# One level of Strassen's scheme for the W product of a conv, low-rank and dense layer, with a reordered opening

## The chip, the cores and the metric

The kernel runs on one core of a Trainium2 chip. The metric is the device time of one execution in microseconds, as the median of several runs. A profile is one execution recorded by the hardware profiler; its span goes from the first to the last instruction on the core.

## The reference

Everything is fp32. A grouped 1-d conv over 64 samples of 64 channels and 1024 positions (4 groups, 16 channels in and out of each, 9 taps, padding 4) gets a term of the condition and a bias; the result, taken as 8 batches of 512 rows of 1024, goes through a dense layer with two low-rank updates, and the input is added.

```python
z   = conv(x, weight) + (cond @ c_weight.T)[:, :, None] + fside[None, :, None]   # (64, 64, 1024)
A   = einsum('bn,nri->bri', gate, lora_A)      # 8 batches, 16 loras, rank 32
B   = einsum('bn,nor->bor', gate, lora_B)
out = x + z @ kernel + bias \
        + (z @ A[b].T) @ B[b].T \
        + (z @ lora_A_shared.T) @ lora_B_shared.T
```

## The kernel before

**Split operands.** TensorE works on fp32r operands. To keep fp32 accuracy each operand is split into a high part (ScalarE copies it into an fp32r tile, `hi_of`, line 104) and a low part (what is left, a subtraction with two SBUF inputs on VectorE or GpSimd, `lo_of`, line 109). A product is three matmuls: high by high, high by low, low by high.

**Tiles.** A row tile is two samples, 128 rows; there are 32, four to a batch. For each tile `load` brings the input in blocks of eight positions, `xhi` and `xlo` split it, `conv` (line 141) runs 24 matmuls of 256 columns, `evac` (VectorE line 159, or ScalarE line 155) adds the condition on the way out of PSUM, `turned` (line 164) transposes 32 by 32 blocks on VectorE so that positions lie on partitions, and `yhi` and `ylo` split the result.

**The W product.** `product` (line 301) multiplies a tile by W in three accumulators of 352, 320 and 352 columns, eight blocks of 128 positions each, three matmuls per block: 72 matmuls. The middle accumulator also carries the 32 rank columns of the batch's low-rank A, so all 72 are 352 wide. The shared low-rank update is folded into W at the start (`fmm`, line 215, on TensorE; `fadd`, line 219, on VectorE).

**The low-rank update of a batch.** `lora_out` copies the 32 rank columns out of PSUM, `turn` (line 312) transposes them on TensorE, `axhi` and `axlo` split them, and `delta` (line 326) adds their product with B, and the bias, to each accumulator. `total` (line 333) adds the residual on VectorE, and `store` writes the tile.

**The mixing of the loras.** A and B of a batch are sums over 16 loras weighted by the gate. `mix` (line 250) does one lora by one VectorE instruction that reads two SBUF tensors; in the opening part of it goes over ScalarE (`gmul`, line 257) and GpSimd (`gadd`, line 261). For each later batch 32 such steps are spread over the tiles of the batch before. B then goes through DRAM (`pbput`, lines 280 and 281, on GpSimd's queue).

**Order.** Each engine issues in program order. Up to the fourth tile the order is the list START, in which W, the loras and the first samples arrive piece by piece. From tile 4 on a loop emits, for tile i, the conv of tile i+1, the store of tile i-1, products, deltas and totals. All loads go over SyncE's queue, the stores over ScalarE's.

Of the kernel before, what the change touches and what calls it, by code (L numbers as in the profile page):

```python
# [8 lines left out]
F32 = mybir.dt.float32  # L9
F32R = mybir.dt.float32r  # L10
ALU = mybir.AluOpType
ACTF = mybir.ActivationFunctionType
PSUM = bass.MemoryType.PSUM

P = 128
NS, C, L = 64, 64, 1024          # samples, channels, length
G, CG, OG, KW = 4, 16, 16, 9     # conv groups, channels in / out of a group, taps
D = 1024                         # output features
NB, NL, R = 8, 16, 32            # batches, loras, rank
NT = NS // 2                     # row tiles: two samples, 128 rows each  # L20
BT = NT // NB                    # row tiles of a batch
JB = 129                         # blocks of 8 positions, half a block off, with padding
CH = ((0, 352), (352, 320), (672, 352))   # columns of W in a tile's three accumulators
CA = 1                           # the accumulator that also carries the lora's R columns
DS = 3 * R                       # rows of the split lora product
NBIAS = 2
NAX = 4
NSTART = 4                       # tiles that the steps of START cover
E = mybir.EngineType
ORDERED = (E.PE, E.SP, E.DVE, E.Activation, E.Pool)  # L30
AW = 8 * R                       # one lora on a partition: 8 x R of A, or 256 of B


# The steps up to the fourth tile, in the order in which each engine issues them: W, the loras and
# the first samples arrive, are split, and are used piece by piece.
START = """
warm, sbload 0, busy 15, busy 6, sbhi 0, sblo 0 v, saload, sahi, cwload, cwide, eye, busy 6, load 0 0 2,
xhi 0 0 2, small 0, twload 2, twload 0, ctload, xlo 0 0 2 p, thi 2, salo, fmm 0 1 m, load 0 2 2, sbload 1,
load 1, thi 0, tlo 0 v, cmul, small 1, xhi 0 2 2, wload 0 0, wload 0 6, wload 0 2, wload 0 4, tlo 2 v,
wload 2 2, xlo 0 2 2 v, small 2, fmm 0 7 m, sbhi 1, sblo 1 p, conv 0 0, conv 0 1, wload 2 6, conv 0 2, xhi 1,  # L40
csum, fmm 0 4 m, evac 0 0 0, conv 0 3, evac 0 1 1, xlo 1 0 4 p, load 2, fmm 0 3 m, wload 2 0, fmm 0 0 m,
fmm 2 6 m, turned 0 0, yhi 0 0 64, fadd 0 1, fadd 0 0, whi 0 0, wload 1 0, fmm 0 6 c, fadd 0 6, ylo 0 0 64 p,
fadd 0 7, lload 0 0 8, fmm 2 0 m, fadd 0 3, whi 0 6, fmm 0 2 c, fadd 0 2, whi 0 2, conv 1 0, turned 0 1,
yhi 0 64 64, wload 2 4, ones, fadd 0 4, fmm 0 5 m, fadd 0 5, fmm 2 7 m, conv 1 1, ylo 0 64 64 p, conv 1 2,
conv 1 3, wload 1 2, whi 0 4, evac 1 0 1, fmm 2 3 m, fmm 1 3 m, wlo 0 0 v, product 0 0 0 2, fadd 2 6,
wlo 0 2 v, fmm 2 5 c, lload 0 8 8, wload 1 6, product 0 0 2 2, fmm 1 1 c, evac 1 1 1, fmm 2 2 m, bihi, xhi 2,
wlo 0 4, wlo 0 6 p, product 0 0 4 2, fadd 2 7, wload 1 4, fmm 2 4 m, xlo 2 0 4 p, product 0 0 6 2, turned 1 0,
turned 1 1, fadd 2 0, yhi 1, fadd 2 3, fadd 1 1, ylo 1 0 128 v, bilo, fmm 2 1 m, fmm 1 0 c, fadd 2 1, whi 2 0,
product 1 0 0 1, fadd 1 0, fadd 2 2, product 1 0 1 2, fmm 1 7 m, mix 0 0 0, mix 0 0 1, product 1 0 3 2,
conv 2 2, product 1 0 5 2, fadd 2 4, product 1 0 7 1, mix 0 0 2, fadd 2 5, fmm 1 2 m, conv 2 0, whi 2 2,  # L50
wlo 2 0 p, product 0 2 0 1, mix 0 0 3, conv 2 1, product 0 2 1 1, whi 2 4, product 1 2 0 1, mix 0 0 4,
lload 1 0 8, mix 0 0 5, fadd 1 3, mix 0 0 6, whi 2 6, fadd 1 2, whi 1 2, evac 2 0 0, conv 2 3, mix 0 0 7,
fadd 1 7, product 1 2 1 1, wlo 2 4 p, mix 0 0 8, wlo 2 2 p, product 0 2 2 1, fmm 1 6 m, mix 0 0 9, mix 0 0 10,
mix 0 0 11, mix 0 0 12, product 1 2 2 1, mix 0 0 13, fmm 1 5 c, wlo 1 2 p, whi 1 0, fadd 1 5, load 3,
wlo 2 6 p, wlo 1 0 p, mix 0 0 14, product 1 2 3 2, gmul 0 1 0, gmul 0 1 3, load 4, mix 0 0 15, fmm 1 4 m,
fadd 1 4, product 0 2 3 5, product 1 2 5 1, fadd 1 6, gmul 0 1 2, gmul 1 1 5, pahi 0, product 1 2 6 2,
palo 0 p, biput 0 1, product 0 1 0 1, xhi 3, residual 0, whi 1 4, mix 1 0 0, total 0 2, mix 1 0 1, gmul 0 1 4,
gmul 0 1 1, wlo 1 4 p, gmul 0 1 5, gmul 0 1 6, product 1 1 0 1, product 0 1 1 2, whi 1 6, xlo 3 0 4 v,
gadd 0 1 1 p, product 1 1 1 2, lload 1 8 8, mix 1 0 2, product 0 1 3 1, product 1 1 3 2, gadd 0 1 2 p,
wlo 1 6 v, evac 2 1 1, turned 2 1, gmul 0 1 10, product 0 1 4 1, product 1 1 5 1, gadd 0 1 3 v,  # L60
product 1 1 6 2, turned 2 0, gmul 0 1 14, gmul 0 1 15, yhi 2, gmul 0 1 8, conv 3 0, conv 3 2, total 0 0,
conv 3 3, gadd 0 1 4 p, gadd 0 1 5 p, gmul 0 1 7, gadd 0 1 6 p, conv 3 1, product 0 1 5 1, gmul 0 1 12,
gmul 0 1 9, gadd 0 1 7 p, product 0 1 6 1, mix 1 0 3, ylo 2 0 128 v, gadd 0 1 8 v, residual 1, product 2 2 0 2,
gmul 1 1 7, product 0 1 7 1, gmul 0 1 11, product 2 1 0 1, mix 1 0 4, product 2 1 1 2, biput 1 1, evac 3 0 0,
product 2 1 3 1, gadd 0 1 9 p, product 2 2 2 3, lora_out 0, turn 0, gmul 0 1 13, product 2 1 4 3,
product 2 0 0 1, gadd 0 1 10 p, gadd 0 1 11 p, evac 3 1 0, turned 3 1, product 2 0 1 1, product 2 1 7 1,
turned 3 0, lora_out 1, gadd 0 1 12 v, gmul 1 1 1, total 0 1, yhi 3, gadd 0 1 13 v, xhi 4, gadd 0 1 14 v,
mix 1 0 5, ylo 3 0 128 p, gmul 1 1 6, product 2 0 2 1, product 2 2 5 1, gadd 0 1 15 v, total 1 1, pbhi 0,
mix 1 0 6, mix 1 0 7, pblo 0 v, axhi 0, axlo 0, mix 1 0 8, mix 1 0 9, gmul 1 1 3, turn 1, total 1 2,
mix 1 0 10, mix 1 0 11, gmul 1 1 4, product 3 1 0 1, gmul 1 1 2, pbput 0, axhi 1, product 3 1 1 1, axlo 1,  # L70
total 1 0, product 3 1 2 1, mix 1 0 12, product 2 2 6 1, product 3 2 0 2, product 2 0 3 1, lora_out 2,
product 3 1 3 1, biput 0 0, product 3 1 4 1, product 2 0 4 1, turn 2, gmul 1 1 0, gmul 1 1 8, axhi 2,
gmul 1 1 14, mix 1 0 13, xlo 4 0 4 v, residual 2, conv 4 0, gmul 1 1 9, gmul 1 1 10, load 5, xhi 5,
product 3 1 5 3, lora_out 3, conv 4 1, gadd 1 1 1 p, gadd 1 1 2 v, gadd 1 1 3 v, gadd 1 1 4 v, gadd 1 1 5 v,
mix 1 0 14, mix 1 0 15, pahi 1, gmul 1 1 13, product 2 0 5 2, axlo 2, product 2 0 7 1, product 2 2 7 1,
delta 2 2, delta 2 0, gadd 1 1 6 p, gadd 1 1 7 p, gmul 1 1 12, gadd 1 1 8 p, conv 4 2, delta 2 1, total 2 0,
total 2 2, product 3 2 2 1, delta 1 2 0, total 1 2, gadd 1 1 9 p, gadd 1 1 10 p, biput 1 0, product 3 0 0 2,
total 2 1, delta 0 1 0, gmul 1 1 11, gadd 1 1 11 p, product 3 0 2 1, gadd 1 1 12 p, gadd 1 1 13 p, gmul 1 1 15,
gadd 1 1 14 p, evac 4 0 1, turn 3, conv 4 3, product 3 0 3 1, axhi 3, axlo 3, turned 4 0, product 3 0 4 1,
delta 3 1, gadd 1 1 15 p, product 3 0 5 1, store 2, delta 0 0 0, total 0 0, pbhi 1, pblo 1 v, product 3 2 3 1,  # L80
evac 4 1 1, product 3 2 4 3, residual 3, turned 4 1, xlo 5 0 4 p, total 3 1, total 0 1, delta 0 2 0, total 0 2,
delta 1 0 0, total 1 0, palo 1 p, pbput 1, yhi 4, product 3 0 6 1, store 0, ylo 4 0 128 v, product 3 2 7 1,
delta 3 2, delta 1 1 0, total 1 1, store 1, total 3 2, product 3 0 7 1, delta 3 0, total 3 0
"""


@with_exitstack
def adaln_ffn(ctx: ExitStack, tc: tile.TileContext, xt, x, tw, w0, w1, w2, la, lb, gt,
              las, lbs, cw, ct, fs, bias, out):
    nc = tc.nc  # L90
    wsrc = (w0, w1, w2)

    const = ctx.enter_context(tc.tile_pool(name="const", bufs=1))
    pcv = ctx.enter_context(tc.tile_pool(name="pcv", bufs=2, space=PSUM))
    pmm = ctx.enter_context(tc.tile_pool(name="pmm", bufs=6, space=PSUM))
    raw = ctx.enter_context(tc.tile_pool(name="raw", bufs=7))
    dram = ctx.enter_context(tc.tile_pool(name="dram", bufs=2, space=bass.MemoryType.DRAM))
    work = ctx.enter_context(tc.tile_pool(name="work", bufs=2))

    def f32(t):  # L100
        return t.bitcast(F32)

    def hi_of(dst, src):
        nc.scalar.copy(dst, src)  # L104

    engs = {"v": nc.vector, "p": nc.gpsimd}

    def lo_of(dst, src, hi, eng="v"):
        engs[eng].tensor_tensor(dst, src, f32(hi), ALU.subtract)  # L109
# [431 lines left out]
```

## Time and profile before

| | |
|---|---|
| time, median of 3 runs | 513.43 us (512.79 to 513.49) |
| span of the profiled execution | 510.9 us |
| its own time | the page gives the span alone; the median of the runs is 2.5 us above it |
| TensorE busy | 497.0 us (97%), granted clock 0.997 |
| VectorE busy | 351.6 us (69%) |
| ScalarE, GpSimd busy | 120.8 and 130.1 us |
| DMA | 67.11 MB, mean 131 GB/s |
| W product, line 301 | 3 x 768 matmuls of 352 columns |
| conv, line 141 | 3 x 256 matmuls of 256 columns |

Busy times of matmuls overlap, since they are pipelined: what one costs is read from the distance between the starts of two.

### The profile page before, as it was taken

To read this page: it belongs to the slowest core of one execution; us is meant where nothing else is said; L and a number is where in the kernel's file an instruction comes from. 1 tells how busy PE (TensorE), PEld (TensorE's weight loads), DVE (VectorE), ACT (ScalarE), POOL (GpSimd) and SP (SyncE) were. 2 spreads that over 40 slices of the span, in tenths; PEclk is the share of its full clock that TensorE was granted. 3 is DMA by queue.
4 is the path that set the end of the run, shared out by engine and by line. 5 is a ranking of instruction groups with operands and counts; after the bars stand their busy time and mean duration, and the time that the engine had idled before them with its cause. 6 is when DMAs were issued, how large, how long until landed. Compare 5 with 4: busy or idle time off the path is not lost.

```text
span 510.9 us, 7936 instructions
## 1 busy us (share of the span) xinstructions
PE 497.0 (97%) x3259; PEld 491.2 (96%) x3259; DVE 351.6 (69%) x572; ACT 120.8 (24%) x221; POOL 130.1 (25%) x93
## 2 busy tenths in 40 slices
PE   8887989999999999999999999999999999999997
PEld 8776989999999999999999999999999999999996
DVE  5999896987737876577846878388864779544321
ACT  5733845111111112101221110211121011211000
POOL 4956538210121113011121102211120111310100
PEclk9998999999999999999999999999999999999999
DMA  8884223813442323333251234322153323441111
GB/s 269 329 335 171 85 87 122 293 77 125 154 156 84 123 83 148 123 125 124 83 182 66 105 125 156 131 107 107 64 181 126 123 84 125 143 166 42 41 42 41
DMA packets 20083, 67.11 MB, mean 131 GB/s; under 512 B 3104, under 2 KB 3840, under 8 KB 19536
## 3 DMA queue, kind: packets, MB, share of 16 engines
q1 hardware_dynamic: 13408, 43.47, 24.4%
q10 hardware_dynamic: 4752, 16.78, 8.2%
q0 software_dynamic: 1888, 6.36, 3.5%
q8 instruction: 25, 0.41, 0.3%
q14 instruction: 10, 0.08, 0.0%
HBM read 46.67 MB, written 19.92 MB: 130 GB/s over the span
## 4 chain that ended last, share of the span: by engine, by line
PE 82%; DVE 6%; POOL 4%; DMA 3%; issue 2%; SPq 2%; ACT 1%; POOLq 0%; ACTq 0%
PE mm L301 63%; PE cv L141 15%; PE mm L326 3%; DMA bst<-bih 2%; DVE eff L250 2%; POOL wl L109 1%; POOL xl L109 1%; DMA sbr<-in_dram 1%; DVE xr L333 1%; DVE z L164 1%; POOL eff L261 1%; PE pt L312 1%; DVE v L159 0%; DVE yl L109 0%; DVE eff L261 0%
## 5 line engine op out<-in xcount | busy, mean ns | idle before, releaser
L301 PE MATMUL mm<-wh,yh 128*128 128x352 f32 x768 | 250.9, 327 | 4.0 <-ACT wh L104 2.8
L301 PE MATMUL mm<-wl,yh 128*128 128x352 f32 x768 | 248.9, 324 | 0.8 <-POOL wl L109 0.8
L301 PE MATMUL mm<-wh,yl 128*128 128x352 f32 x768 | 248.7, 324 | 0.0
L301 PEld LDWEIGHTS mm<-wh,yh 128*128 128x128 f32 x768 | 144.9, 189 | 5.9 <-ACT wh L104 3.1
L301 PEld LDWEIGHTS mm<-wl,yh 128*128 128x128 f32 x768 | 145.0, 189 | 1.8 <-POOL wl L109 1.7
L301 PEld LDWEIGHTS mm<-wh,yl 128*128 128x128 f32 x768 | 144.8, 189 | 0.1
L250 DVE SCALAR_TENSOR_TENSOR eff<-lora,gat,eff 128x256 f32<-128x256 f32 x210 | 140.3, 718 | 0.5
L109 POOL TENSOR_TENSOR xl<-xt,xh 128x1032 fp32r<-128x1032 f32 (+1 forms) x30 | 74.9, 2497 | 249.8 <-ACT xh L104 249.7
L333 DVE TENSOR_TENSOR xr<-mm,xr 128x352 f32<-128x352 f32 (+1 forms) x96 | 46.3, 509 | 77.4 <-PE mm L326 77.4
L104 ACT CAST yh<-z 128x1024 fp32r<-128x1024 f32 (+1 forms) x33 | 33.8, 1025 | 240.8 <-DVE z L164 240.8
L159 DVE TENSOR_TENSOR v<-cv,cadd 128x512 f32<-128x512 f32 x58 | 40.0, 690 | 20.6 <-PE cv L141 20.4
L141 PE MATMUL cv<-xl,th 128*128 128x256 f32 x256 | 51.6, 282 | 1.6 <-DVE xl L109 1.0
L141 PE MATMUL cv<-xh,th 128*128 128x256 f32 x256 | 51.6, 283 | 0.7 <-DVE wr L219 0.7
L141 PE MATMUL cv<-xh,tl 128*128 128x256 f32 x256 | 51.4, 282 | 0.0
L164 DVE STREAM_TRANSPOSE z<-v 128x512 f32<-128x512 f32 x64 | 45.2, 709 | 2.1 <-ACT v L155 0.2
L109 DVE TENSOR_TENSOR yl<-z,yh 128x1024 fp32r<-128x1024 f32 x30 | 37.6, 1253 | 13.0 <-ACT yh L104 12.5
L141 PEld LDWEIGHTS cv<-xh,th 128*128 128x128 f32 x256 | 40.9, 189 | 1.3 <-DVE wr L219 1.2
L141 PEld LDWEIGHTS cv<-xl,th 128*128 128x128 f32 x256 | 39.5, 189 | 2.0 <-DVE xl L109 1.3
L141 PEld LDWEIGHTS cv<-xh,tl 128*128 128x128 f32 x256 | 39.5, 189 | 0.0
L104 ACT CAST xh<-xt 128x1032 fp32r<-128x1032 f32 (+1 forms) x33 | 33.9, 1027 | 1.1 <-DMA xt<-in_dram 1.1
L109 DVE TENSOR_TENSOR axt<-pt,axt 32x128 fp32r<-32x128 f32 x32 | 9.2, 288 | 28.1 <-ACT axt L104 27.5
L326 PE MATMUL mm<-bst,axt 98*128 98x352 f32 (+1 forms) x90 | 24.0, 319 | 0.2 <-DVE axt L109 0.2
(56 smaller groups left out, 216.1 us busy)
## 6 DMA issues: line engine op xcount, KB each, us to landing
xr<-in_dram SPq DMA_DIRECT2D x32, 512.0 KB, 4.4
xt<-in_dram SPq DMA_DIRECT2D x31, 516.0 KB, 3.6
out_dram<-xr ACTq DMA_DIRECT2D x31, 512.0 KB, 2.6
lora<-in_dram SPq DMA_DIRECT2D x4, 1024.0 KB, 6.3
bsc<-bhl POOLq DMA_DIRECT2D x8, 384.0 KB, 3.8
bst<-bsc POOLq DMA_DIRECT2D x8, 384.0 KB, 3.5
wr<-in_dram SPq DMA_DIRECT2D x8, 352.0 KB, 7.3
wr<-in_dram SPq DMA_DIRECT2D x4, 320.0 KB, 3.2
```

What stands on the lines that cost most here:

```text
L104: nc.scalar.copy(dst, src)
L109: engs[eng].tensor_tensor(dst, src, f32(hi), ALU.subtract)
L141: nc.tensor.matmul(cps[i, hf][:, gg], a[:, kt, g, :], b[:, g, :, kt:kt + P], start=(n == 0), stop=(n == len(prods) - 1))
L159: nc.vector.tensor_tensor(v[:, g0:g0 + 2], ps, c.unsqueeze(3).to_broadcast([P, 2, 2, P]), ALU.add)
L164: nc.vector.transpose(z[:, :, hf * 64:hf * 64 + 64].rearrange("p k (m o) -> p m k o", o=OG), v[:, g0:g0 + 2].rearrange("p g n j -> p (g n ...
L250: nc.vector.scalar_tensor_tensor(e, lora[w][:, n], gat[:, n, b:b + 1], e, ALU.mult, ALU.add)
L261: engs[eng].tensor_tensor(e, e, gated.pop((b, w, n)), ALU.add)
L301: nc.tensor.matmul(ps[:, :m], a[:, k, :], b[c][:, k, :m], start=(k == 0 and q == 0), stop=(k == 7 and q == 2))
L312: nc.tensor.transpose(pts[i], axs.pop(i).rearrange("p a r -> p (a r)"), ident)
L326: nc.tensor.matmul(acc[i, c][:, :n], axt[i % NAX], bst[(i // BT) % 2][:, c0:c0 + n], start=not more, stop=True, skip_group_check=bool(more))
L333: nc.vector.tensor_tensor(o, acc.pop((i, c))[:, :n], o, ALU.add)
```

## The change

**Pairs and blocks.** Two row tiles form a pair. The 256 by 1024 matrix of a pair and the 1024 by 1024 W are cut into 2 by 2 blocks, and the eight block products become seven (Winograd's variant): four sums of blocks of the pair (`asum`, GpSimd), four of W, made once (`wsum`, both engines), and seven products (`prod`), each four blocks of 128 positions by three matmuls of 512 columns. The products accumulate in four PSUM banks; three times a bank is copied out in between (`keep`, ScalarE), and the copies are added to the residual (`xsum`, `ysum`, `radd`, `yadd`) before `total`. All seven left and seven right blocks are split into high and low parts.

**The rest.** `conv` takes a pair and one group at a time, 512 columns instead of 256. The low-rank input is computed turned: the batch's A is the stationary operand and 128 positions by 128 rows of the pair the moving one (`lora`), so the TensorE transpose goes, and the accumulators carry no rank columns. The gate's mixing is done once at the start for all batches: per lora tensor eight fp32 matmuls with a masked gate (`gmask`, `mix`), copied out by ScalarE (`mixout`), written to DRAM (`mixput`) and read back per batch (`aload`, `bload`). GpSimd's queue issues only two small loads. Loads and stores become smaller and more.

**Order.** One list, ORDER, of 1657 steps replaces START and the loop. In its opening (up to `prod 2 0`) the seven products of pairs 0 and 1 are cut into single blocks and follow the arrival and preparation of W.

```diff
-CH = ((0, 352), (352, 320), (672, 352))   # columns of W in a tile's three accumulators
+A11, A12, S1, S3, A22, S2, S4 = range(7)
+B11, B21, T1, T3, N4, T2, B22, B12 = range(8)
+PRODUCTS = ((A11, B11, "a"), (A12, B21, "a"), (S1, T1, "d"), (S3, T3, "c"), (A22, N4, "c"), (S2, T2, "b"),
+            (S4, B22, "d"))
+ORDER = """
+warm, twload 0, gload, small 1, busy 26, saload 0, twload 1, small 0, xload 0 0, cwload, ctload, xload 0 1,
...
+conv 1 3, gmask, xhi 2 0, turned 1 0, wsum 3 2 p, wload 6 0, prod 0 3 0 1 0, evac 1 2 v, whi 3 2, wload 7 0,
+turned 1 1, xlo 2 0 p, prod 0 3 1 1 0, xhi 2 1, turned 1 2, evac 1 3 a, xload 2 2, conv 2 0, fadd 4 0,
+wlo 3 2 p, lload 0 2, wsum 3 3 v, mix 0 0, evac 2 0 a, fadd 6 0, xlo 2 1 p, prod 0 3 2 1 0, fadd 5 0, whi 3 3,
...
+rload 5 1, asum 5 5, delta 4 1, keep 5 0, lora 5 0, total 4 1, delta 4 3, asum 5 6, yhi 5 4, conv 6 0,
+total 4 3, store 4 1, rload 5 3, ylo 5 4 v, store 4 3, prod 5 1, xhi 6 2, evac 6 0 v, xlo 6 2 v, turned 6 0,
+xload 7 0, bload 3 0, lora 5 1, conv 6 1, yhi 5 5, bload 3 1, ylo 5 5 v, prod 5 2, xhi 6 3, evac 6 1 v,
+xlo 6 3 v, turned 6 1, xload 7 1, lora 5 2, keep 5 2, conv 6 2, yhi 5 6, ylo 5 6 v, prod 5 3, xhi 7 0,
+evac 6 2 v, xlo 7 0 v, turned 6 2, xload 7 2, conv 6 3, yhi 6 0, keep 5 3, ylo 6 0 v, lora 5 3, ysum 5 v,
+xhi 7 1, prod 5 4, axlow 5, evac 6 3 v, xlo 7 1 p, ahi 3, axsum 5, turned 6 3, axhi 5, xload 7 3, axlo 5,
+alo 3 p, prod 5 5, yhi 6 1, asum 6 2, aload 4, ylo 6 1 v, asum 6 3, delta 5 0, yhi 6 2, xsum 5, prod 5 6,
+adiff 4 p, total 5 0, radd 5 2 v, radd 5 1 p, store 5 0, radd 5 3 v, delta 5 2, ylo 6 2 v, yadd 5 p, yhi 6 3,
...
+    def conv(p, g):
+        h, l = xsp.pop((p, g))
+        ps = cps[p, g] = pcv.tile([P, 4, P], F32, tag="cv", name=f"cv{p}_{g}")
+        prods = [(kt, a, b) for a, b in ((th, h), (tl, h), (th, l)) for kt in range(2)]
+        for n, (kt, a, b) in enumerate(prods):
+            nc.tensor.matmul(ps, a[:, kt, g, :], b[:, :, kt:kt + P],
+                             start=(n == 0), stop=(n == len(prods) - 1))
...
+    def asum(p, b, eng="p"):
+        t = raw[p, b] = slot("s", f"s{b}_{p}", (P, HK, P))
+        m, n, op = {S1: (quarter(p, 1, 0), quarter(p, 1, 1), ALU.add),
+                    S2: (raw.get((p, S1)), quarter(p, 0, 0), ALU.subtract),
+                    S3: (quarter(p, 0, 0), quarter(p, 1, 0), ALU.subtract),
+                    S4: (quarter(p, 0, 1), raw.get((p, S2)), ALU.subtract)}[b]
+        engs[eng].tensor_tensor(t, m, n, op)
...
+    def wsum(b, k, eng="p"):
+        t = wr[b, k] = piece(f"ws{b}_{k}")
+        m, n = {T1: (B12, B11), T3: (B22, B12), T2: (B22, T1), N4: (B21, T2)}[b]
+        engs[eng].tensor_tensor(t, wr[m, k], wr[n, k], ALU.subtract)
...
+    def mix(w, i, pool="m"):
+        pl, tag = {"m": (pmm, "mm"), "c": (pcv, "cv")}[pool]
+        mps[w, i] = pl.tile([NB * GC, 2 * AW], F32, tag=tag, name=f"mx{w}_{i}")
+        nc.tensor.matmul(mps[w, i], gm.rearrange("p b i -> p (b i)"), lraw[w, i], start=True, stop=True)
...
+    def prod(p, j, k0=0, nk=HK, alone=0):
+        ab, bb, to = PRODUCTS[j]
...
+        h, l = spl[p, ab]
+        for k in range(k0, k0 + nk):
+            for q, (a, b) in enumerate(((h, wh), (h, wl), (l, wh))):
+                s = first and k == 0 and q == 0
+                nc.tensor.matmul(ps, a[:, k, :], b[bb, k], start=s, stop=(k == HK - 1 and q == 2),
+                                 skip_group_check=not first)
...
+    def lora(p, b):
+        hf, blk, k0 = ((0, A11, 0), (0, A12, HK), (1, S1, 0), (1, A22, 2 * HK))[b]
+        ps = axp[:, p % 2, hf, :]
+        h, l = spl[p, blk]
+        s = sta[p // BP]
+        for k in range(HK):
...
+            both = lambda **f: nc.tensor.matmul(ps, s[:, k0 + k].rearrange("p q r -> p (q r)"), h[:, k, :], **f)
+            one = lambda **f: nc.tensor.matmul(ps[0:R], s[:, k0 + k, 0, :], l[:, k, :], **f)
...
+    def keep(p, j):
+        t = cop[p, j] = slot("c", f"c{j}_{p}")
+        nc.scalar.copy(t, acc[p, PRODUCTS[j][2]])
...
+    def radd(p, b, eng="p"):
+        r = res[p, b]
+        engs[eng].tensor_tensor(r, r, cop[p, "x"], ALU.add)
...
+    def biput(n):
+        nc.sync.dma_start(f32(bst[DS + n:DS + n + 1, :]).rearrange("o (p d) -> o p d", p=P), f32(bih[:, n, :]))
```

In ORDER the numbers after `prod` are pair, product, first block, blocks and whether it has a bank of its own; those after most other steps are the pair and the group or block; a final `p` or `v` says GpSimd or VectorE, and `a` ScalarE.

## Prediction

> **What bounds the kernel now.** I read the page's busy times first, then the chain, then the spacing of matmuls in the timeline, last VectorE and GpSimd in the opening.
>
> ```profile
> span 510.9 us, 7936 instructions
> PE 497.0 (97%) x3259; PEld 491.2 (96%) x3259; DVE 351.6 (69%) x572; ACT 120.8 (24%) x221; POOL 130.1 (25%) x93
> ...
> DVE  5999896987737876577846878388864779544321
> ...
> PE 82%; DVE 6%; POOL 4%; DMA 3%; issue 2%; SPq 2%; ACT 1%; POOLq 0%; ACTq 0%
> ```
>
> TensorE carries 82% of the chain. VectorE's row is near 9 only in the first slices, so there are two stages. The chain in order of time shows the second:
>
> ```profile
> 465.26 2.88 PE cv L141 x24
> 468.14 5.76 PE mm L301 x36
> ...
> 480.29 2.86 PE cv L141 x24
> ...
> 507.47 0.53 DVE xr L333
> ```
>
> A tile takes 480.29 - 465.26 = 15.03 us. Counted back, tile 4 begins at 90.0: an opening of 90.0, 27 tiles of 15.0, a last tile without conv (12.1), and 3.5 us after the last matmul. The timeline gives the price of a matmul:
>
> ```profile
> 300.68 0.40 PE L141 MATMUL cv<-xh,th 128*128 128x256 f32 x2
> 300.92 0.40 PE L141 MATMUL cv<-xh,tl 128*128 128x256 f32 x2
> ...
> 303.14 0.32 PE L301 MATMUL mm<-wh,yl 128*128 128x352 f32 x1
> 303.30 0.32 PE L301 MATMUL mm<-wh,yh 128*128 128x352 f32 x1
> ...
> 308.58 0.27 PE L312 MATMUL pt<-ident,axs 128*96 128x128 f32 x1
> 308.61 0.41 PE L301 MATMUL mm<-wh,yh 128*128 128x352 f32 x1
> 308.85 0.32 PE L301 MATMUL mm<-wl,yh 128*128 128x352 f32 x1
> ```
>
> Start to start, over all such rows: 256 columns 119.5 ns, 320 columns (delta) 146.6, 352 columns 160.5; the fp32 transpose of 128 columns 270 - 160 = 107. A tile: 72 x 0.1605 + 24 x 0.1195 + 0.47 of deltas + 0.11 = 15.0. TensorE is gapless there. In the opening it is not:
>
> ```profile
> 0.00:90.00 90.00, 79.79 (x489) 75.59 (x490) 75.65 (x118) 48.11 (x100) 56.67 (x54) 0.98 0.58 200
> ```
>
> (PE, PEld, DVE, ACT, POOL busy.) By spacing, TensorE has 73 us of work in these 90. The reason is here:
>
> ```profile
> 17.60 1.56 POOL L109 TENSOR_TENSOR yl<-z,yh 128x512 fp32r<-128x512 f32 x1
> ...
> 18.35 1.56 DVE L109 TENSOR_TENSOR wl<-wr,wh 128x704 fp32r<-128x704 f32 x1
> ...
> 22.72 1.53 DVE L109 TENSOR_TENSOR yl<-z,yh 128x1024 fp32r<-128x1024 f32 x1
> 23.11 3.39 POOL L109 TENSOR_TENSOR xl<-xt,xh 128x1032 fp32r<-128x1032 f32 x1
> ...
> 24.16 2.36 DVE L109 TENSOR_TENSOR bih<-bia,bih 128x8 fp32r<-128x8 f32 x1
> ```
>
> A VectorE subtraction of 8 elements takes 2.36 us: it ends when GpSimd's ends. VectorE operations with two SBUF inputs and GpSimd's exclude each other; those with a PSUM input keep their time. So these two kinds form one queue, which I call the shared port. From the moment the other lets go: VectorE 704 columns 0.75 us (19.16 to 19.91), so 0.55 for 512 and 1.1 for 1032; GpSimd 1032 columns 2.25 (24.25 to 26.50), 704 in 1.58, so 1.16 for 512. Between 10 and 75 us one or the other held it in 54.7 of 65 us (84%), and VectorE, waits included, was busy 94%.
>
> **The stretch after the opening.** A pair now has 7 x 4 x 3 = 84 product matmuls, 24 of conv and 4 deltas, all 512 wide. The rows rise by 0.43 ns a column, which gives 160.5 + 160 x 0.43 = 229 ns; bounds are 239 (two of 256) and 227 (the idle products at half clock, 213.3 ns for 256, halved per column). I take 229, nearest to the 352 row.
>
> The 32 `lora` matmuls move 128 columns with 64 or 32 weight columns. No row shows that. The line through the rows gives 119.5 - 128 x 0.43 = 64.5 ns; the other end is `cmul`'s rows (line 402: 64 moving, 128 weight columns), 112 ns apart. I take 64.5, since the weights are half as wide.
>
> Here the Trainium skill speaks against the change: "TensorE: Matmul & The Clock Gate", Back-to-back issue gap, puts a stream at 81 ns for 128 columns and 131 for 512. By it `lora` would cost 7 us more in all. But its 131 lies below the 160 measured here for only 352 columns, so the rows decide.
>
> A pair: 84 x 0.229 = 19.24, conv 5.50, deltas 0.92, `lora` 2.06: 27.7 us against 30.0 for two tiles. From the first instruction of `prod 2 0`: 14 pairs x 20.16 = 282.2; 12 convs 66.0 (those of pairs 0 to 3 stand in the opening); 440 `lora` matmuls 28.4; five deltas left over 1.1. Sum 377.7. After the last matmul three totals of 0.68 (line 333 scaled to 512) instead of one: 3.5 + 1.3 = 4.8.
>
> Can the others keep up? VectorE per pair: evacuations 4 x 0.69, transposes 4 x 0.71, totals 4 x 0.68, `xsum`, `axsum`, `axlo` 1.5, and about 15 subtractions and additions with two SBUF inputs, 10.3 alone (0.68 for 512, 1.23 for 1032): 19.7. The 210 mixing steps of line 250 (140 us) are gone, which pays for this. GpSimd: four `asum`, one or two each of `ylo` and `xlo`, one or two additions: 12 us. Port: 20.5 of 27.7. Since every step with two SBUF inputs may meet a GpSimd operation, VectorE loses some 4 to 6 us: 24 to 26 of 27.7. It fits, and the left operands are asked for two or three products (5 to 8 us) ahead. ScalarE has 14 us. Loads fall to 264 KB in pieces of 1 KB, twice as many on SyncE's queue; DMA engines are at 0.32 of their time, so I cost this at nothing; were it exposed, a landing took 3.6 us. `keep` has 1.9 us of conv and `lora` before its bank is written again; without that cover, 0.6 us three times a pair.
>
> **The opening.** TensorE: 96 conv 22.0, 168 product matmuls 38.5, 16 `fmm` 3.7, 26 idle products 5.5, `cmul` and deltas 1.6, 72 `lora` 4.6, 16 `mix`. A `mix` is fp32, 512 wide; the trace shows `cmul` recorded as two matmuls each, and a transpose pass at 107 ns per 128 columns: 2 x 4 x 107 = 0.86 us, 13.7 in all (bounds 7, two passes at 0.229, and 29, `cmul` per column). Sum 89.6.
>
> The port: VectorE 55 operations of 512 (22 `wlo`, 16 `ylo`, 8 `wsum`, others) at 0.55, 9 `xlo` at 1.1, two small: 41. GpSimd 34 of 512 (12 `asum`, 8 `wsum`, 6 `wlo`, others) at 1.16, 9 `xlo` at 2.27, small ones 2.5: 62. Together 103, against some 64 in the old opening. That exceeds TensorE's 89.6, so the port sets the end of the opening. The last 6 us (`adiff`, `alo`, pair 4's `xlo`) are not needed by `prod 2 0`. The first such operation comes at about 4 us. With the 84% of the old opening: 4 + 97 / 0.84 = 119.5. From the other side: TensorE's work by the old ratio, 89.6 x 90 / 73 = 110; VectorE's unblocked work (64 became 90 before), 85.7 x 90 / 64 = 120; the port's by the same ratio, 103 x 90 / 64 = 145; gapless, 4 + 97 = 101. I take 120, which two of these give. `mixput` waits on SyncE's queue for ScalarE's copy, with the next lora and x loads behind it; `biput` (up to 10.7 us to land before) stands ahead of W's second half. I cost both at nothing, since the port is the later one: half of its load lies after them.
>
> **The sum.** 120 + 377.7 + 4.8 = 502.5 against the span of 510.9. The median lies 2.5 above that span: 505. The break-even opening is 510.9 - 4.8 - 377.7 = 128.4.
>
> **The rivals.** *The port chokes the opening.* VectorE and GpSimd each issue in order, so a blocked subtraction also holds up evacuations and transposes behind it, TensorE waits for these, and idle stretches bring half clock (the trace has one at 47 us). By 145 the time is 530. It decides from 128 on. For it: the old opening lost 17 us to this with two thirds of the load. Against: more of VectorE's other work (36 us) can run under GpSimd's. *The pair does not stay TensorE-bound.* VectorE at 24 to 26 of 27.7 plus its waits for the port becomes the bound: 29.5 a pair adds 14 x 1.8 = 25, so 530. It decides from 0.6 us a pair on. Against: 5 to 8 us of lead. *The port is packed.* TensorE and port end near 103: 488. *The change does not do what it says* at 239 ns a matmul: 16 us more, 521.
>
> **How the numbers follow.** Forecast (495 to 514) 0.50; packed opening 0.16; choked opening 0.17; pair bound by VectorE, or 239 ns, 0.17. The range 489 to 527 leaves about 2 in 10 out: part of the packed case, part of the slower two. A measurement of this kernel tells 0.2% (1 us) from no change. Faster: 0.16 and nine tenths of 0.50, with little of the slower cases, 0.64; same 0.04; slower 0.32.
>
> **What would show it.** 512-wide matmuls 229 ns apart; `lora` 64; `prod 7 0` to `prod 8 0` 27.7 us; `prod 2 0` at 120 with the port held above 80% before it; TensorE at 9 from there on. The prediction is wrong if the opening passes 128, or if TensorE waits inside a pair for a VectorE or GpSimd subtraction.

## Result: 1.81 times as slow, and the profile after

The changed kernel took 928.13 us (median of 4 runs, 927.61 to 928.82), the kernel before beside it 513.46 us: a ratio of 1.8066, with a 95% interval of 1.8026 to 1.8107. The forecast was 505, with a range of 489 to 527. These lines of the page of the changed kernel already say which kind of miss this is:

```profile
span 926.2 us, 6941 instructions
...
PE 537.8 (58%) x2386; PEld 416.1 (45%) x2386; DVE 367.0 (40%) x491; ACT 201.9 (22%) x402; POOL 247.0 (27%) x186
...
PE   8688848162557084843839157573558439496800
...
PEclk9899969585869588876879669695788768798865
DMA  8662211111121212212121121212122121211111
...
DMA 53%; PE 23%; DVE 8%; SPq 5%; issue 4%; ACTq 2%; ACT 2%; POOL 1%; DVEq 0%; POOLq 0%
DMA xt<-in_dram 29%; DMA r<-in_dram 13%; DMA out_dram<-r 9%; PE mm_d L490 5%; PE mm_a L490 5%; PE mm_c L490 4%; SPq L533 3%; PE mm_b L490 2%; PE cv L274 2%; ACTq L575 2%; DVE y L241 1%; DVE r L556 1%; DMA wr<-in_dram 1%; DVE r L572 1%; PE mx L424 1%
```

No engine is the bound: TensorE, 97% busy before, is at 58%, and VectorE at 40%. The chain is 53% DMA, where it was 3%. Yet the row of DMA shows one or two tenths from the fourth slice on. Transfers that are waited for, on DMA engines that are idle for the most part, are the contradiction to resolve. The granted clock (0.788 on the mean) is lowest where TensorE waits: 5 to 8 tenths in the slices with TensorE at 5 tenths or less, 8 or 9 in the others (rows PE and PEclk).

The view of the waits names engines first, and only then a DMA (waiter, line, releaser: us in total, times, longest):

```profile
POOL xs L241 <- ACT xs L236: 446.6, 16, 46.9
ACT xs L236 <- DMA xt<-in_dram: 342.2, 27, 35.0
DVE xs L241 <- ACT xs L236: 281.9, 22, 34.2
PEld mm_c L490 <- ACT c L537: 220.4, 12, 31.4
PE mm_c L490 <- ACT c L537: 218.1, 12, 31.3
```

TensorE waits 218 us for ScalarE's `keep` (L537). The copy itself takes 0.58 us; it stands in ScalarE's queue behind `xhi` (L236), and that waits 342 us for the input. The timeline shows the queues between 398 and 425 us (start, us, engine; an SPq line is SyncE issuing a transfer; [idle before, releaser]):

```profile
398.12 4.90 SPq L533 DMA_DIRECT2D r<-in_dram  x1
...
403.12 9.95 SPq L257 DMA_DIRECT2D xt<-in_dram  x1
...
413.12 11.89 SPq L533 DMA_DIRECT2D r<-in_dram  x3
423.52 0.62 ACT L236 CAST xs<-xt 128x516 fp32r<-128x516 f32 x1 [24.09 <-DMA xt<-in_dram]
...
424.57 0.58 ACT L537 COPY c<-mm_c 128x512 f32<-128x512 f32 x1
...
425.20 0.80 PE L490 MATMUL mm_c<-wh,y 128*128 128x512 f32 x1 [20.37 <-ACT c L537]
```

SyncE takes 2.4 to 9.95 us to issue one entry here (the 11.89 us are three); in experiment e5 below it takes 0.3 to 0.6 us for most. The x load behind a residual load, issued at 403 us, is there at 423.5. The chain in order of time (start, us) has such landings from the opening on:

```profile
103.37 23.55 DMA r<-in_dram x2
...
159.36 21.13 DMA r<-in_dram
181.24 21.08 DMA out_dram<-r
```

On the chain such transfers, and loads of x queued behind them, mostly took 14 to 25 us. In the kernel before, a residual load of twice the size landed in 4.4 us, a load of x in 3.6 (its page, KB each and median us from issue to landing):

```profile
xr<-in_dram SPq DMA_DIRECT2D x32, 512.0 KB, 4.4
xt<-in_dram SPq DMA_DIRECT2D x31, 516.0 KB, 3.6
```

The reason is in two steps that the forecast passed over, `rload` (L533) and `store` (L575):

```python
def xrow(t, p, b):
    hf, h = divmod(b, 2)
    return t.rearrange("(i h r) d -> i h r d", h=2, r=64)[2 * p:2 * p + 2, hf, :, HN * h:HN * h + HN]
...
nc.sync.dma_start(res[p, b], xrow(x, p, b))                 # rload
nc.scalar.dma_start(xrow(out, p, b), res.pop((p, b)))       # store
```

A block's 128 rows are two runs of 64, so the DRAM side of these transfers is 2 x 64 x 512. Counted in the trace between 398 and 430 us, packets of 2048 B (there only these transfers have them) go through at 24 to 26 in almost every microsecond, loads and stores together, and each takes 84 ns: 25 x 0.084 = 2.1 engines at work, of 16. The x load issued at 403 us is not confined, and still waits for those two engines: 224 of its 256 packets pass between 413.7 and 415.1 us, the last 32, two sixteenths, only at 422.2 to 423.0. The count of packets says the same (first the changed kernel, then e5, where each of these transfers is 128 x 512):

```profile
DMA packets 50322, 66.99 MB, mean 72 GB/s; under 512 B 4080, under 2 KB 31728, under 8 KB 50288
DMA packets 52114, 66.99 MB, mean 131 GB/s; under 512 B 5872, under 2 KB 33520, under 8 KB 52080
```

The 1792 packets that are missing are all of 4 bytes: 14 for each of the 128 residual loads and stores, which is what one closing packet per engine gives if 2 engines work on a transfer instead of 16. All residual loads and stores are 2 x 8192 packets: 16384 x 0.084 / 2 = 688 us of work for two engines, and a sixteenth of the time of all other packets, some 125 us, is theirs too (an estimate, if those spread evenly). The Trainium skill states the rule behind this ("DMA: Bandwidth & Descriptors", Why a DMA increments its semaphore by 16 and not by 1): a transfer goes to the largest number of engines, up to 16, that divides the slowest dimension larger than 1 of both its access patterns. The 2.1 engines counted here agree; the forecast did not weigh it.

By stage, the changed kernel beside the version of experiment e5 below, which differs from it only in that layout:

| stage | forecast | changed kernel | e5 |
|---|---|---|---|
| opening, to the start of `prod 2 0` | 120 | 145.4 | 118.9 |
| from there to the last matmul | 377.7 | 736.5 | 386.3 |
| after the last matmul | 4.8 | 44.3 | 4.9 |
| span | 502.5 | 926.2 | 510.1 |

### The profile page after: what moved, and what is told of

Its sections match the earlier page's. It is cut to its first block, busy times and chain, and to the rows that moved or that the text cites. A ratio compares the mean times of both kernels' runs of the same rounds, so it can differ in the third digit from the quotient of the medians.

```text
span 926.2 us, 6941 instructions
## 1 busy us (share of the span) xinstructions
PE 537.8 (58%) x2386; PEld 416.1 (45%) x2386; DVE 367.0 (40%) x491; ACT 201.9 (22%) x402; POOL 247.0 (27%) x186
## 4 chain that ended last, share of the span: by engine, by line
DMA 53%; PE 23%; DVE 8%; SPq 5%; issue 4%; ACTq 2%; ACT 2%; POOL 1%; DVEq 0%; POOLq 0%
DMA xt<-in_dram 29%; DMA r<-in_dram 13%; DMA out_dram<-r 9%; PE mm_d L490 5%; PE mm_a L490 5%; PE mm_c L490 4%; SPq L533 3%; PE mm_b L490 2%; PE cv L274 2%; ACTq L575 2%; DVE y L241 1%; DVE r L556 1%; DMA wr<-in_dram 1%; DVE r L572 1%; PE mx L424 1%
## 5 line engine op out<-in xcount | busy, mean ns | idle before, releaser
L490 PE MATMUL mm_c<-wh,y 128*128 128x512 f32 x256 | 107.5, 479 | 218.1 <-ACT c L537 218.1
L490 PEld LDWEIGHTS mm_c<-wh,y 128*128 128x128 f32 x256 | 60.1, 235 | 240.7 <-ACT c L537 220.4
L236 ACT CAST xs<-xt 128x516 fp32r<-128x516 f32 x64 | 39.8, 624 | 396.8 <-DMA xt<-in_dram 342.2
L490 PE MATMUL mm_a<-wh,y 128*128 128x512 f32 x256 | 91.7, 415 | 46.7 <-ACT c L537 35.4
L274 PE MATMUL cv<-xs,th 128*128 128x512 f32 x256 | 86.2, 421 | 12.1 <-ACT xs L236 11.8
L490 PE MATMUL mm_d<-wh,y 128*128 128x512 f32 x240 | 86.0, 416 | 0.0
L490 PEld LDWEIGHTS mm_a<-wh,y 128*128 128x128 f32 x256 | 51.3, 200 | 60.0 <-ACT c L537 36.5
L236 ACT CAST y<-s 128x512 fp32r<-128x512 f32 x64 | 39.7, 620 | 119.6 <-DVE r L572 58.5
L490 PE MATMUL mm_c<-wl,y 128*128 128x512 f32 x128 | 59.9, 468 | 0.0
L274 PEld LDWEIGHTS cv<-xs,th 128*128 128x128 f32 x256 | 48.4, 199 | 22.7 <-ACT xs L236 13.2
L490 PE MATMUL mm_a<-wl,y 128*128 128x512 f32 x128 | 52.6, 411 | 0.0
L490 PE MATMUL mm_d<-wl,y 128*128 128x512 f32 x120 | 49.7, 414 | 0.0
```

What stands on the lines that cost most here:

```text
L274: nc.tensor.matmul(ps, a[:, kt, g, :], b[:, :, kt:kt + P], start=(n == 0), stop=(n == len(prods) - 1))
L490: nc.tensor.matmul(ps, a[:, k, :], b[bb, k], start=s, stop=(k == HK - 1 and q == 2), skip_group_check=not first)
```

## The experiments

Two theories stood at first. **Two engines:** the outer dimension of 2 confines each residual load and store to two DMA engines. **The rivals:** SyncE's queue is overloaded by the number of loads; or the packets of 2 KB, or the scattered rows, cost the time; or the order of steps leaves too little lead, whatever the transfers do.

### e1: each transfer as two of 64 rows

```diff
-        nc.sync.dma_start(res[p, b], xrow(x, p, b))
+        for i in range(2):
+            nc.sync.dma_start(res[p, b][64 * i:64 * i + 64], xrow(x, p, b)[i])
...
-        nc.scalar.dma_start(xrow(out, p, b), res.pop((p, b)))
+        r = res.pop((p, b))
+        for i in range(2):
+            nc.scalar.dma_start(xrow(out, p, b)[i], r[64 * i:64 * i + 64])
```

> The changed kernel with each residual load and each output store written as two transfers of 64 rows by 512 columns instead of one whose DRAM side is 2 by 64 by 512. Theory (the outer dimension of 2 puts such a transfer on two DMA engines; trace after: 25 packets of 2 KB a us at 84 ns each is 2.1 engines busy): the 8192 + 8192 packets, 688 us of two engines, spread over sixteen, the stretch becomes TensorE-bound, r loads land in under 5 us, time 495 to 515. Rival (2 KB pieces and the number of transfers on the queues are what is slow): pieces keep their size and the transfers double, time stays above 850.

520.95 us (520.08 to 521.57), 1.0143 times the kernel before [1.0126, 1.016]. Bytes, packet size, order of steps and engine work are those of the changed kernel, and both queues issue more transfers: SyncE's rival, the 2 KB packets and the lead that the order leaves are refuted as the cause. The time lies above the 495 to 515 that was expected. Residual loads land in 3.2 us:

```profile
DMA  8989412415744362526453453527252644334223
...
PE 73%; DVE 11%; DMA 6%; issue 4%; SPq 2%; ACT 1%; ACTq 1%; POOL 0%; DVEq 0%; POOLq 0%
...
r<-in_dram SPq DMA_DIRECT2D x128, 128.0 KB, 3.2
out_dram<-r ACTq DMA_DIRECT2D x128, 128.0 KB, 2.6
```

TensorE carries the chain again, and the DMA row has risen, for the same bytes in little over half the time. Beside e5 below, e1 loses 3.3 us in the opening, 4.0 us in the stretch (from `prod 3 0` to `prod 5 0` its pairs take 29.1 and 29.9 us, later ones 28.2) and 2.1 us at the end, where the half stores stretch it to 7.0 us.

### e2 and e3: only one of the two

e2 has the edit of `rload` alone, e3 that of `store` alone.

> Only the residual loads are split into two of 64 rows; the stores keep the outer dimension of 2. Two-engine theory: 8192 store packets of 84 ns on two engines are 344 us, under the span, so the time comes near the fully split kernel but keeps stalls where loads queue behind stores on these engines: 510 to 600. Rival (pieces, number of transfers): above 850.

> Only the stores are split; the residual loads keep the outer dimension of 2. Two-engine theory: again 344 us of two engines, but on SyncE's queue, in front of the x loads, which need all sixteen engines: 520 to 650, worse than splitting the loads. Rival (pieces, number of transfers): above 850.

One run each: e2 656.49 us, e3 682.97 us. Both halves matter, the loads a little more, in the order expected; but both lie above their ranges, so half the load on two engines hurts more than I thought. The 8192 packets left are 344 us of work for two engines, which would fit under 510 if only the mean counted. It doesn't: as with the x load above, the other transfers need those two engines as well, and whoever waits for one waits for its last packets. In e2 the largest part of the chain goes over the stores that stayed in the old form:

```profile
DMA out_dram<-r 40%; DMA xt<-in_dram 8%; PE mm_d L490 6%; PE mm_a L490 4%; PE mm_c L490 4%; DMA r<-in_dram 4%; PE mm_b L490 2%; SPq L463 2%; PE mx L424 2%; DVE r L573 2%; SPq L534 1%; POOL s L316 1%; PE cv L274 1%; DMA wr<-in_dram 1%; DMA sbr<-in_dram 1%
```

### e4, e8, e9: the outer dimension alone, in the kernel before

If the shape does it, the kernel before must suffer from it too, without anything of Strassen's scheme. Its residual loads and stores get an outer dimension of 2 (shown), 4 or 16. Bytes, packet size and number of transfers stay; since nothing else is changed to match, the residual is added, and the result stored, at other rows than the reference's.

```diff
+    def two(t, i):
+        return t.rearrange("(i h r) d -> i h r d", h=2, r=64)[i & ~1:(i & ~1) + 2, i & 1]
...
-        nc.sync.dma_start(xrs[i], x[i * P:(i + 1) * P, :])
+        nc.sync.dma_start(xrs[i], two(x, i))
...
-        nc.scalar.dma_start(out[i * P:(i + 1) * P, c0:c0 + n], xrs[i][:, c0:c0 + n])
+        nc.scalar.dma_start(two(out, i)[:, :, c0:c0 + n], xrs[i][:, c0:c0 + n])
```

> The kernel before, with its residual load and its store given the outer dimension of 2: the tiles of a pair take rows 0 to 63, or 64 to 127, of both tiles, so rows of the residual and of the output stand in other places; bytes, pieces (4 KB) and the number of transfers stay. Two-engine theory: 2 x 128 packets of 159 ns on two engines are 20.4 us a tile where TensorE needs 15.0, so 32 x 20.4 = 651 plus what the opening does not hide: 640 to 700. Rival (pieces of 2 KB, number of transfers): nothing changes, 511 to 516.

> The kernel before, with residual loads and stores whose DRAM side has an outer dimension of 4 (4 x 32 rows x 1024, the rows of four tiles interleaved) in place of the 2 x 64 x 1024 that took 738.0 us; the rows of the residual and of the output stand in other places. If the outer dimension sets the number of DMA engines: four engines share 8192 packets of 4 KB, at 159 ns each 8192 x 0.159 / 4 = 326 us of work in 510 us, so they are no longer the bound. A residual lands in about 32 x 0.159 = 5 us, and transfers queued behind it come later, with one tile in hand: 512 to 530 us, 515 likeliest. If the scattered rows or the three-dimensional pattern cost the time, and not the number of engines: near 738 us.

> The same with an outer dimension of 16 (16 x 8 rows x 1024, sixteen tiles interleaved): more scattered than the last, with the same number and size of packets. If the outer dimension sets the number of DMA engines: all 16 work, and the time is that of the kernel before, 512 to 516 us. If scatter costs the time: near 738 us or above.

| outer dimension | time, us | ratio to before | 4 KB packets in a microsecond, while they queue | 4 KB packets at work at once, most often | 4-byte packets fewer than before |
|---|---|---|---|---|---|
| 2 x 64 (e4) | 738.04, one run | | 12 to 14 | 2 | 910 = 65 x 14 |
| 4 x 32 (e8) | 525.82 (524.64 to 527.08) | 1.0239 [1.0202, 1.0276] | 25, up to 28 | 4 | 780 = 65 x 12 |
| 16 x 8 (e9) | 518.91 (515.62 to 520.85) | 1.0091 [1.0057, 1.0125] | up to 69 | 16 | none |
| 128 rows at a stretch (before) | 512.97 | 1 | up to 99 | 16 | |

The packets are those of SyncE's and ScalarE's queues from 100 to 480 us; 65 is the number of residual loads and stores. A packet of 4 KB takes 159 ns, so 13 of them in a microsecond are 13 x 0.159 = 2.07 engines. More scatter with as many packets gives a shorter time: what decides is the outer dimension. The rows cut into the most pieces cost 6 us, those cut into the fewest 225. e4 lies above its range of 640 to 700, as two engines have 8192 x 0.159 / 2 = 651 us of these packets, and their share of all other packets, some 100 us (an estimate, if those spread evenly), comes on top. e9 lies 3 us above its range. Its 4 KB packets take 204 ns in the median instead of 159, and its residual loads land in 5.6 us against 4.4. Its profiled execution also has one wait of TensorE of 3.9 us at 102 us, before a delta, for which the profile shows no releaser; what ties it to the loads is left open. In e4 the final addition of the residual waits for the loads, which the kernel before doesn't show among its longest waits:

```profile
DVE xr L336 <- DMA xr<-in_dram: 205.8, 18, 16.5
```

### e5: the changed kernel with other rows together

The host lays out the residual and the output so that the 128 rows of a block lie one after another; each transfer is then 128 x 512.

```diff
-        return t.rearrange("(i h r) d -> i h r d", h=2, r=64)[2 * p:2 * p + 2, hf, :, HN * h:HN * h + HN]
+        return t[(2 * p + hf) * P:(2 * p + hf + 1) * P, HN * h:HN * h + HN]
```

> The changed kernel with the residual's and the output's rows laid out in memory so that the 128 rows of a block follow one another: each residual load and each store stays one transfer, now 128 by 512 on both sides, 64 of each. Two-engine theory: all sixteen engines, as with the split transfers, without the doubled count: 508 to 521, and a shorter end than the 7.0 us that eight half stores left after the last matmul. Rival (the number of transfers or the piece size costs): as many 2 KB pieces as in the changed kernel, so 850 and more.

512.03 us, median of 12 runs (one of them took 2691.66 us and is not in the ratio), against 513.32: 0.9978 [0.996, 0.9996]. One line of layout is worth 416 us. What is left is the change that the forecast had thought it was costing, and it is 0.2% faster than the kernel before, an interval that ends just below 1. Its page answers the one shown of before:

```profile
span 510.1 us, 6941 instructions
...
PE 488.8 (96%) x2386; PEld 382.9 (75%) x2386; DVE 381.0 (75%) x491; ACT 204.8 (40%) x402; POOL 245.8 (48%) x186
...
PE   8889679989999999999999999999999999999996
...
PE 77%; DMA 9%; DVE 6%; issue 2%; SPq 2%; POOL 1%; ACT 1%; DVEq 0%; POOLq 0%; ACTq 0%
```

### e6 and e7: what sets the opening

With the transfers mended, the opening (118.9 us against 90.0) takes back what the pairs gain. Was it the shared port that the forecast named, or simply VectorE's own work? e6 moves 14 opening steps (eight `wsum`, six `wlo`) from GpSimd to VectorE, where each holds the port for half as long; e7 moves 22 `wlo` the other way.

```diff
-... wsum 3 0 p, ... wlo 3 0 p, ... wsum 3 1 p, ...        (e6, 14 such steps)
+... wsum 3 0 v, ... wlo 3 0 v, ... wsum 3 1 v, ...
-... wlo 5 0 v, ... wlo 5 1 v, ... wlo 5 2 v, ...          (e7, 22 such steps)
+... wlo 5 0 p, ... wlo 5 1 p, ... wlo 5 2 p, ...
```

> As e5_rows, and in the opening the 14 steps of wsum and wlo that GpSimd does are given to VectorE. If the port that both share sets the opening (14 x (1.16 - 0.55) = 8.5 us less of port time, at 84% coverage): prod 2 0 comes about 10 us sooner, time 10 us less than e5_rows. If VectorE's own load sets it (14 x 0.68 = 9.5 us more, times 1.4): prod 2 0 about 13 us later, time 13 us more.

> As e5_rows, and in the opening the 22 wlo that VectorE does are given to GpSimd. If the shared port sets the opening (22 x 0.61 = 13.4 us more of port time at 84%): prod 2 0 about 16 us later. If VectorE's own load sets it (15 us less, times 1.4): up to 21 us sooner.

| | e6 | e5 | e7 |
|---|---|---|---|
| time, us | 510.22 (509.84 to 511.38) | 512.03 | 518.60 (517.73 to 518.79) |
| ratio to before | 0.9941 [0.9919, 0.9963] | 0.9978 [0.996, 0.9996] | 1.0095 [1.007, 1.0119] |
| start of `prod 2 0` | 117.4 | 118.9 | 126.9 |
| port held, of 105 us (10 to 115) | 80.0 | 85.4 | 95.3 |
| VectorE busy, of the same 105 | 94.3 | 90.5 | 72.1 |

The sign is the port's in both, and against VectorE's own work: giving VectorE more makes the opening shorter (by 1.6 us only), taking work off it makes it longer. The size is not: +8.0 us for a port theory's 16, and -1.6 for its 10. In e6 the freed port goes unused, while VectorE is busy for 94.3 of 105 us. That speaks for the port and VectorE setting the opening together, and for little more to be had from moving these steps between the two; no run frees both at once, so it is argued and not shown. e6 is the fastest kernel of this study, 0.6% below the kernel before.

## Why the prediction was wrong

**The step that failed** is one sentence: "Loads fall to 264 KB in pieces of 1 KB, twice as many on SyncE's queue; DMA engines are at 0.32 of their time, so I cost this at nothing". It prices the loads of x, whose form had become finer but stayed wide. Residual loads and stores were not priced at all. And "0.32 of their time" is a mean over 16 engines; a transfer that can use only two has an eighth of what the mean seems to leave free. Its bound from above, "were it exposed, a landing took 3.6 us", took the landing time from transfers of another shape; on the chain the new ones, and x behind them, mostly took 14 to 25 us. None of the rivals contained this. The step is worth 416 us (926.2 - 510.1), and e5 shows it whole.

**The opening.** In the changed kernel `prod 2 0` starts at 145.4 us, to the microsecond where the rival "The port chokes the opening" had put it. That is a coincidence: the chain there goes through two residual loads, the 23.55 us from 103.37 on shown above, and with these mended the opening is 118.9, for a forecast of 120. A number that fits a rival does not confirm its mechanism. Counted as the forecast counted the old opening, the port is held for 85.4 of 105 us in e5, 81% for its 84%, and for 24.5 of 25.0 us from 50 to 75. Up to `prod 2 0` that is 92.2 us where the forecast had 97: less work at a lower share. With e6 and e7, which moved the opening by less than a port alone would, 118.9 so near 120 is in part luck. Two steps of e5 there show the forecast's price of a subtraction (start, us, engine):

```profile
58.74 1.77 POOL L316 TENSOR_TENSOR s<-z 128x512 f32<-128x512 f32 x1
59.25 1.80 DVE L241 TENSOR_TENSOR y<-s,y 128x512 fp32r<-128x512 f32 x1
```

GpSimd lets go at 60.51, VectorE ends at 61.05: 0.54 us alone, for a forecast of 0.55. The Trainium skill ("SBUF — State Buffer", Who interferes with whom) calls this port pair an exclusive lock; these rows agree.

**The pairs.** In e5 the timeline shows the new shapes:

```profile
299.73 0.40 PE L490 MATMUL mm_c<-wh,y 128*128 128x512 f32 x1
299.97 0.40 PE L490 MATMUL mm_c<-wl,y 128*128 128x512 f32 x1
300.21 0.62 PE L490 MATMUL mm_c<-wh,y 128*128 128x512 f32 x2
300.67 0.39 PE L490 MATMUL mm_c<-wl,y 128*128 128x512 f32 x1
...
303.23 0.22 PE L501 MATMUL axp<-y,sta 128*64 128x128 f32 x1
303.29 0.22 PE L502 MATMUL axp<-y,sta 128*32 128x128 f32 x1
303.35 0.22 PE L501 MATMUL axp<-y,sta 128*64 128x128 f32 x1
```

The distance of product matmuls is 232 ns in the median and 234.5 on the mean (forecast 229), of conv matmuls 235 and 239.7 (229), of `lora` 60 (64.5). The rival of 239 ns came half true: the products lie midway to it, the convs reach it. A pair takes 28.2 us, not 27.7. The stretch is 386.3, not 377.7, and the means explain the 8.6: products 1176 x 5.5 ns = 6.5, conv 288 x 10.7 ns = 3.1, `lora` -2.0, deltas 0.9. The rival in which VectorE becomes the bound of a pair did not come: TensorE was busy for 385.2 of these 386.3 us. The end took 4.9 us for 4.8. So 229 ns was too low, the second term that missed, by 8.6 us in all.

**The sum.** So the forecast's own terms, where the transfers are wide, gave a span of 502.5 and e5 510.1. Its time of 512.03 lies in the forecast's range, and the sign is right by 0.2%, which is no more than a close call. The gain is so small because what the pairs save, 31.1 us (417.4 from tile 4 to the last matmul before, 386.3 now), goes into the longer opening, 28.9, and the longer end, 1.4.

**Slips in the working.** Half of 213.3 ns per column gives 213 for 512 columns, not the lower bound of 227; VectorE's terms for a pair add up to 20.1, not 19.7; and by the count that gave 54.7 of 65 us the port is held for 73.2 us in the old opening, not some 64, which turns the 145 reached by that ratio into 127. None of them carries the forecast.

**What of the named tests caught it.** "The prediction is wrong if the opening passes 128, or if TensorE waits inside a pair for a VectorE or GpSimd subtraction." The opening did pass 128, and TensorE did wait inside the pairs, but mostly for ScalarE's copy, and behind it for a DMA.

## What to carry to other kernels

For every transfer that a change touches, write down both access patterns and look at the outermost dimension before its bytes: 2 x 64 rows and 128 rows move the same data, and here 416 us lay between them. Free time of the DMA engines in the mean says nothing about a transfer that can use only some of them; a page with DMA on the chain, a low DMA share and slow landings is its mark. Where an in-order engine stands between, follow a wait on to what its queue was blocked by.

## What was not expected of the hardware

- Transfers with an outer dimension of 2 worked on 2.1 engines by their packets (25 x 84 ns in a microsecond; 13 x 159 ns in e4), those of 4 on 4.0 (25 x 159 ns in e8), and the issuing queue slowed with them: SyncE's issues took 2.4 to 9.95 us around 410 us in the changed kernel, 0.3 to 0.6 us for most in e5.
- A transfer that can use all engines still waits for the two: 224 of an x load's 256 packets passed by 415.1 us, the last 32 at 422.2 to 423.0.
- Half the packets on two engines, 344 us of work in a kernel of some 510, still cost 135 and 162 us (e2 and e3 against e1).
